# Storing a spectrum by component, mode and line instead of line, component and mode

## The chip, the cores and the metric

The program runs on one core of one Trainium2 chip. The metric is device time in microseconds of one execution of the whole program, from the first to the last instruction. A core has several engines that run side by side, each with its own in-order queue: TensorE (PE in the profile, with its weight loads shown as PEld), VectorE (DVE), ScalarE (ACT), GpSimd (POOL) and SyncE (SP, which here only starts transfers). Engines wait for one another through semaphores. Matmuls read their two operands from the on-chip memory SBUF and write to the accumulators in PSUM; VectorE and ScalarE read and write both.

## The reference, cut to what matters

Four layers follow one another on an input of 4 images of 64 x 64 pixels with 128 channels; each adds its result to its input. The change is in the second one, layer 1 in the code. It normalizes by groups of four channels, takes a real Fourier transform along each of the two image axes, keeps 16 modes, multiplies each mode by its own complex 128 x 128 channel matrix, transforms back, and sends the sum through a two-stage feed-forward with a layer norm:

```python
def _forward_fourier(x, w1, w2):
    xt = jnp.transpose(x, (0, 3, 1, 2))
    ...
    fty = jnp.fft.rfft(xt, axis=-1, norm='ortho')
    f1 = jnp.einsum('bixy,ioy->boxy', fty[..., :nm], cw1)      # nm = 16 modes
    xy = jnp.fft.irfft(jnp.concatenate([f1, pad_y], axis=-1), n=N, axis=-1, norm='ortho')
    ftx = jnp.fft.rfft(xt, axis=-2, norm='ortho')
    f2 = jnp.einsum('bixy,iox->boxy', ftx[:, :, :nm, :], cw2)
    xx = jnp.fft.irfft(jnp.concatenate([f2, pad_x], axis=-2), n=M, axis=-2, norm='ortho')
    return jnp.transpose(xx + xy, (0, 2, 3, 1))
h = _forward_fourier(x, w1, w2)
h1 = jax.nn.relu(jnp.einsum('bmni,ih->bmnh', h, ff_w0) + ff_b0)
h2 = jnp.einsum('bmnh,ho->bmno', h1, ff_w1) + ff_b1
return _layer_norm(h2, ln_g, ln_b)
...
x = x + _L1_conv_ref(_gn(x), L1_conv_w1, L1_conv_w2, ...)
```

## The kernel before, in words

The layers run one after the other. `layer1` loops over the four images and calls `layer1_image` for each. All data is fp32. Layer 0 has a queue of work with due times and layer 2 has a planner, but in layer 1 the order of the work on each engine is that of the program as the tile framework lays it out, with pools of buffers deciding what may run ahead. After the first image the weights of layer 2 are prepared (`layer2_weights`, L744 and following); the framework moves many of these small VectorE operations between those of image 0's second axis.

For one image, `layer1_image` finds the scale `s_` and offset `o_` of the group norm (`group_norm`, transposes at L59), and then does the same for each of the two axes. I call that a half image; there are eight. A line is one of the 64 rows (or columns) of the image. A half image goes like this:

- **Analysis, L641.** 32 matmuls, four to a PSUM tile `pu`. Each takes 128 pixels (two lines) as weights and streams the 96 columns of the transform table `an`, which hold sine, cosine and minus sine of 16 modes for both lines. So a `pu` tile holds eight lines, each with 3 x 16 = 48 values, for 128 channels on the partitions. The three components let one complex product be done as two real matmuls.
- **Write of the spectrum, L642.** ScalarE scales each `pu` tile by `s_` and writes it to `U`. There are eight such writes, straight through: both sides have 384 adjacent floats. `U` has one buffer of the shape line, component, mode.
- **Correction, L645.** VectorE adds eight times the offset to the 64 values of the cosine component of mode 0.
- **Mode products, L653 and L656.** For each of 16 modes two matmuls accumulate in PSUM: the weights are the real and the imaginary channel matrix of this mode, and two components of `U` for all 64 lines stream through, 128 columns. Four modes fill one PSUM tile `pg`.
- **Copy, L659.** VectorE copies `pg` to `G`, in the order line, mode, component. Four copies.
- **Back transform, L665 to L684.** TensorE transposes `G` (L665), ScalarE copies the result (L667), TensorE multiplies it with the synthesis table (L671), and VectorE puts the result into `hT` (L681) or adds it there (L684).

After both axes come the feed-forward (L691, L692, L696) and the layer norm (from L701), in eight blocks of 512 pixels, and the store at L716. The second axis reads the image a second time with the pixels in column order (`xa`, L636).

PSUM tiles come from a pool with two tags, `a` and `b`, of four buffers each. `pu` and `pt` share `a`; `pg`, `ph` and `po` share `b`.

Of the kernel before, what the change touches and what calls it, by code (L numbers as in the profile page):

```python
# [11 lines left out]
F32 = mybir.dt.float32  # L12
AF = mybir.ActivationFunctionType
ALU = mybir.AluOpType
# [3 lines left out]
P = 128  # L18
# [65 lines left out]
def layer0(sh, A, x_in, x_out, scr):  # L84
# [7 lines left out]
    with ExitStack() as ctx:  # L92
# [300 lines left out]
        def products(G, q, hT):  # L393
            U = G["unit"]
            rev = U["rev"]
            qo = 3 - q if rev else q
            e = qo // 2
            if U["yT"][e] is None:
                U["yT"][e] = psy.tile([P, 2, 2 * P], F32, name=f"yT{e}")
                if U["k"] == 0:  # L400
                    for r in range(2):
                        for s in range(2):
                            t0 = (2 * e + r) * P
                            nc.tensor.matmul(
                                U["yT"][e][:, r, s * P : (s + 1) * P],
                                lhsT=U["u"][:, s, t0 : t0 + P],
                                rhs=D_diag[:, s, :],
                                start=(r == 0 and s == 0),
                                stop=False,
                                skip_group_check=True,  # L410
                            )
                    U["started"] |= {(e, j) for j in range(4)}
            for j in range(4):
                jo = 3 - j if rev else j
                nc.tensor.matmul(  # L415
                    U["yT"][e][32 * jo : 32 * jo + 32, qo % 2, :],
                    lhsT=U["Ws"][G["g"]][:, :, 4 * q + j],
                    rhs=hT[:, j, :],
                    start=((e, jo) not in U["started"]),
                    stop=(G["g"] == 3),  # L420
                    skip_group_check=True,
                )
                U["started"].add((e, jo))
            if G["g"] == 3 and q % 2:

                y, k = U["y"], U["k"]
                ye = y[:, 2 * e : 2 * e + 2, :]
                if k == 1:
                    nc.scalar.copy(ye, U["yT"][e])
                else:  # L430
                    nc.vector.tensor_tensor(ye, ye, U["yT"][e], ALU.add)  # L431
                if k == 2:
                    for r in range(2):
                        nc.vector.bn_stats(U["st"][:, 4 * U["pc"] + 2 * e + r, 0, :], y[:, 2 * e + r, :])
                if q == 3:
                    nc.sync.dma_start(U["dst"](k), y)
# [179 lines left out]
def layer1_image(sh, w, pools, x_dram, x_out, x=None):  # L616

    nc = sh.nc
    big, tmp, small, ps = pools
    if x is None:  # L620
        x = big.tile([P, NJ, DM], F32, name="x1")
        load_image(nc, x, x_dram)
    s_, o_ = sh.group_norm(lambda j: x[:, j, :], ps, small, tag="a")
    o8 = small.tile([P, 1], F32, name="o8")
    nc.vector.tensor_scalar(o8, o_, 8.0, None, ALU.mult)

    hT = big.tile([P, NT], F32, name="hT", bufs=1)
    for axis in range(2):

        if axis == 0:  # L630
            xa = x
        else:
            xa = big.tile([P, NJ, DM], F32, name="xa", bufs=1)
            xv = x_dram.rearrange("(h w2 w1) d -> w1 h w2 d", w1=2, w2=32)
            for q in range(2):
                nc.sync.dma_start(xa[64 * q : 64 * q + 64], xv[q])  # L636
        U = tmp.tile([P, 64, 3, 16], F32, name="U1", bufs=1)
        for g in range(NJ // 4):
            pu = ps.tile([P, 4 * 96], F32, name="pu", tag="a")
            for q in range(4):  # L640
                nc.tensor.matmul(pu[:, q * 96 : q * 96 + 96], lhsT=xa[:, 4 * g + q, :], rhs=w["an"], start=True, stop=True)  # L641
            nc.scalar.activation(  # L642
                U[:, 8 * g : 8 * g + 8].rearrange("p l c m -> p (l c m)"), pu, AF.Identity, scale=s_
            )
        nc.vector.tensor_scalar(U[:, :, 1, 0], U[:, :, 1, 0], o8, None, ALU.add)  # L645

        G = tmp.tile([P, 64, 16, 2], F32, name="G1", bufs=1)
        wm = w["w1"] if axis == 0 else w["w2"]
        for g in range(4):
            pg = ps.tile([P, 4, 2, 64], F32, name="pg", tag="b")  # L650
            for q in range(4):
                m = 4 * g + q
                nc.tensor.matmul(  # L653
                    pg[:, q], lhsT=wm[:, m, 0, :], rhs=U[:, :, 1:3, m].rearrange("p l c -> p c l"), start=True, stop=False
                )
                nc.tensor.matmul(  # L656
                    pg[:, q], lhsT=wm[:, m, 1, :], rhs=U[:, :, 0:2, m].rearrange("p l c -> p c l"), start=False, stop=True
                )
            nc.vector.tensor_copy(G.rearrange("p l m c -> p m c l")[:, 4 * g : 4 * g + 4], pg)  # L659

        for g in range(4):
            pt = ps.tile([P, 4, P], F32, name="pt", tag="a")
            for q in range(4):
                l0 = 4 * (4 * g + q)
                nc.tensor.transpose(pt[:, q, :], G[:, l0 : l0 + 4].rearrange("p l m c -> p (l m c)"), sh.ident)  # L665
            GT = tmp.tile([P, 4, P], F32, name="GT1")
            nc.scalar.copy(GT, pt)  # L667
            for q in range(0, 4, 2):
                ph = ps.tile([P, 8, 64], F32, name="ph", tag="b")
                for e in range(2):  # L670
                    nc.tensor.matmul(  # L671
                        ph[:, 4 * e : 4 * e + 4, :].rearrange("p l t -> p (l t)"),
                        lhsT=GT[:, q + e, :],
                        rhs=w["sy"],
                        start=True,
                        stop=True,
                    )
                l0 = 4 * (4 * g + q)
                hv = hT.rearrange("p (h w) -> p h w", w=64)
                if axis == 0:  # L680
                    nc.vector.tensor_copy(hv[:, l0 : l0 + 8, :], ph)  # L681
                else:
                    hv = hv.rearrange("p h w -> p w h")[:, l0 : l0 + 8, :]
                    nc.vector.tensor_tensor(hv, hv, ph, ALU.add)  # L684


    for c in range(NCH):
        h1 = tmp.tile([P, 4, CH], F32, name="h1")
        for f in range(4):
            pf = ps.tile([P, CH], F32, name="pf", tag="a")  # L690
            nc.tensor.matmul(pf, lhsT=w["ff0"][:, f, :], rhs=hT[:, c * CH : (c + 1) * CH], start=True, stop=True)  # L691
            nc.scalar.activation(h1[:, f, :], pf, AF.Relu, bias=w["b0"][:, f : f + 1])  # L692
        po = ps.tile([P, 4, DM], F32, name="po", tag="b")
        for q in range(4):
            for f in range(4):
                nc.tensor.matmul(  # L696
                    po[:, q, :], lhsT=h1[:, f, q * P : (q + 1) * P], rhs=w["ff1"][:, f, :], start=(f == 0), stop=(f == 3)
                )
        row = lambda n: w["rows"][:, n, :].unsqueeze(1).to_broadcast([P, 4, DM])
        h2 = tmp.tile([P, 4, DM], F32, name="h2")  # L700
        nc.vector.tensor_tensor(h2, po, row(0), ALU.add)  # L701
        st = small.tile([P, 4, 6], F32, name="ln_st")
        mv = small.tile([P, 4, 2], F32, name="ln_mv")
        for q in range(4):
            nc.vector.bn_stats(st[:, q, :], h2[:, q, :])
            nc.vector.bn_aggr(mv[:, q, :], st[:, q, :])
        r = sh.rstd(small, mv[:, :, 1], [P, 4], "ln_r")
        for q in range(4):
            nc.vector.tensor_scalar(
                h2[:, q, :], h2[:, q, :], mv[:, q, 0:1], r[:, q : q + 1], ALU.subtract, ALU.mult  # L710
            )
        nc.vector.tensor_tensor(h2, h2, row(1), ALU.mult)
        nc.vector.tensor_tensor(h2, h2, row(2), ALU.add)
        xc = x[:, 4 * c : 4 * c + 4, :]
        nc.vector.tensor_tensor(xc, xc, h2, ALU.add)
        nc.sync.dma_start(x_out[c * CH : (c + 1) * CH, :].rearrange("(j p) d -> p j d", p=P), xc)  # L716


def load_image(nc, x, x_dram):
    for q in range(4):  # L720
        nc.sync.dma_start(
            x[:, 8 * q : 8 * q + 8, :], x_dram[1024 * q : 1024 * q + 1024, :].rearrange("(j p) d -> p j d", p=P)
        )
# [1120 lines left out]
```

## Time and profile before

The time is 8232.35 us, the median of three executions (8224.83, 8232.35, 8241.54).

| | whole program | second layer |
|---|---|---|
| stretch of the span | 0 to 8232.3 us | 6050 to 6610 us |
| TensorE busy | 6551.1 us (80%) | 507.2 us |
| TensorE weight loads | 4166.6 us (51%) | 418.1 us |
| VectorE busy | 6752.2 us (82%) | 294.6 us |
| ScalarE busy | 6192.0 us (75%) | 149.6 us |
| GpSimd busy | 5481.8 us (67%) | 0.0 us |
| mean granted TensorE clock | 0.95 | 0.94 |
| data moved | 142 GB/s | 43 GB/s |

A busy time is a sum over instructions, and matmuls overlap in their pipeline: what one matmul costs in a stream is read from the distance of the starts, not from its length. "PEclk" is the granted clock of TensorE as a share of full speed. "Idle before" says how long an engine stood still before a group of instructions and what released it. A row of the timeline merges instructions that follow one another on one line; "x2" means two records. Each fp32 matmul leaves two records, so a half image has 64 records of mode products.

The layer begins, after a short stretch for the group norm, at TensorE's first analysis matmul at 6050.7 us. In the first half image ScalarE writes the eight parts of U between 6052.8 and 6061.1 us, VectorE corrects mode 0 at 6061.08, the mode products run from 6061.42 to 6075.7, and the fourth G copy follows at 6075.73.

### The profile page before, as it was taken

What the parts mean: (1) busy time and instruction counts of PE and PEld (TensorE: products, weight loads), DVE (VectorE), ACT (ScalarE), POOL (GpSimd) and SP (SyncE); (2) the same over time, 40 slices, a digit from 0 to 9 for tenths busy, and PEclk for the clock granted to TensorE, in tenths of its full rate; (3) what the DMA queues carried; (4) which work ended last, traced back from release to release, by engine and by line L of the source; (5) the groups of instructions that cost most, each with busy time, mean ns of one, the idle gap of its engine ahead of it and who ended that gap; (6) DMA issues with size and microseconds to landing.
All of it is one profiled execution on the core that took longest, in us unless ns stands there. A gap on an engine that the chain in (4) does not pass through costs nothing.

```text
span 8232.3 us, 141196 instructions
## 1 busy us (share of the span) xinstructions
PE 6551.1 (80%) x52976; PEld 4166.6 (51%) x52976; DVE 6752.2 (82%) x7948; ACT 6192.0 (75%) x9798; POOL 5481.8 (67%) x2502
## 2 busy tenths in 40 slices
PE   7788888778888777888887777787778978587689
PEld 3344454444445444444544444454457756474456
DVE  2889999998999999889999999999944554635778
ACT  3899999988898898989988999999822222414567
POOL 0889899998888898888888999999900011020233
PEclk9899999999999999999999999999989989798799
DMA  6445555545555554555555445555541132330332
GB/s 122 158 146 185 162 170 176 162 158 153 183 168 173 179 171 156 159 169 168 173 177 178 163 154 178 177 176 177 174 92 47 25 97 64 83 106 20 108 94 79
DMA packets 1403839, 1165.69 MB, mean 142 GB/s; under 512 B 759829, under 2 KB 1197681, under 8 KB 1336210
## 3 DMA queue, kind: packets, MB, share of 16 engines
q1 hardware_dynamic: 1401474, 1154.93, 45.5%
q8 instruction: 417, 6.83, 0.3%
q14 instruction: 268, 2.20, 0.1%
q10 hardware_dynamic: 1680, 1.74, 0.1%
HBM read 962.66 MB, written 189.74 MB: 140 GB/s over the span
## 4 chain that ended last, share of the span: by engine, by line
PE 21%; DVE 11%; ACT 10%; issue 3%; DMA 2%; POOL 2%; SPq 1%; ACTq 0%; DVEq 0%; POOLq 0%
DVE h L493 5%; ACT hT L390 4%; ACT dA L492 3%; PE pt L380 2%; POOL dB L486 1%; PE po L696 1%; PE pf L691 1%; PE pz L884 1%; PE pt L1527 1%; PE pu L884 1%; DVE in_st L884 1%; PE pb L884 1%; DVE m L884 1%; PE pa L884 1%; PE ps L1581 1%
## 5 line engine op out<-in xcount | busy, mean ns | idle before, releaser
L493 DVE TENSOR_TENSOR_SCAN h<-dA,state,dB 128x512 f32<-128x512 f32 x4096 | 4960.2, 1271 | 340.3 <-ACT dA L492 211.7
L486 POOL TENSOR_TENSOR dB<-du,Bb 128x1024 f32<-128x1024 f32 x2048 | 4816.7, 2386 | 524.5 <-DVE h L493 381.6
L380 PE MATMUL pt<-ident,h 128*128 128x128 f32 x16384 | 2245.1, 281 | 993.4 <-ACT hT L390 988.5
L492 ACT ACTIVATE dA<-delta,A_neg 128x512 f32<-128x512 f32 x4096 | 2746.0, 690 | 166.3 <-DVE h L493 139.4
L380 PEld LDWEIGHTS pt<-ident,h 128*128 128x128 f32 x16384 | 1836.1, 142 | 2029.6 <-ACT hT L390 1783.0
L390 ACT COPY hT<-pt 128x1024 f32<-128x1024 f32 x2048 | 2068.8, 1010 | 187.3 <-PE pt L380 170.8
L415 PE MATMUL yT<-hT,W 128*32 128x256 f32 x16384 | 1394.7, 413 | 2.7 <-DVE y L431 2.1
L884 POOL COPY XG<-Xs 64x9 f32<-64x9 f32 (+2 forms) x44 | 10.9, 293 | 1016.6 <-ACT Xs L884 1016.5
L415 PEld LDWEIGHTS yT<-hT,W 128*32 128x32 f32 x16384 | 454.1, 150 | 350.9 <-issue 333.8
L215 PE MATMUL cv<-xn,taps 128*128 128x512 f32 x1152 | 613.3, 633 | 0.0
L1565 POOL TENSOR_TENSOR S<-S,sm 128x784 f32<-128x784 f32 x128 | 191.1, 1493 | 432.4 <-DVE sm L1563 248.4
L326 PE MATMUL dp<-xd,w_dt 65*128 65x512 f32 x512 | 296.2, 661 | 106.1 <-ACT Ct L313 92.5
L335 POOL TENSOR_TENSOR du<-delta,u 128x1024 f32<-128x1024 f32 x128 | 304.9, 2382 | 66.1 <-DVE delta L332 66.1
L215 PEld LDWEIGHTS cv<-xn,taps 128*128 128x128 f32 x1152 | 183.5, 188 | 234.4 <-issue 233.0
L307 PE MATMUL xd_ps<-u,w_x 128*48 128x512 f32 x512 | 251.1, 614 | 41.3 <-DMA u<-l_xw 16.2
L1572 ACT ACTIVATE S<-S,mx 128x196 f32<-128x196 f32 x512 | 227.9, 448 | 34.8 <-DVE mx L1599 34.2
L692 ACT ACTIVATE h<-pf,b 128x512 f32<-128x512 f32 x128 | 88.0, 687 | 146.6 <-PE pf L691 146.6
L332 DVE SCALAR_TENSOR_TENSOR delta<-delta,dp 128x512 f32<-128x512 f32 x256 | 169.5, 662 | 24.2 <-ACT delta L330 24.2
L326 PEld LDWEIGHTS dp<-xd,w_dt 65*128 65x128 f32 x512 | 78.2, 192 | 218.4 <-ACT Ct L313 151.1
L329 ACT ACTIVATE delta<-dp 128x512 f32<-128x512 f32 x256 | 152.4, 595 | 24.2 <-PE dp L326 19.3
L330 ACT ACTIVATE delta<-delta 128x512 f32<-128x512 f32 x256 | 162.4, 635 | 8.1
L1527 PE MATMUL pt<-ident,S 128*98 128x128 f32 x1024 | 165.3, 286 | 3.3 <-POOL S L1565 1.9
(344 smaller groups left out, 6929.3 us busy)
## 6 DMA issues: line engine op xcount, KB each, us to landing
Bb<-l_B SPq DMA_DIRECT2D x512, 1024.0 KB
W<-l_W SPq DMA_DIRECT2D x512, 256.0 KB
l_y<-y SPq DMA_DIRECT2D x128, 512.0 KB
u<-l_xw SPq DMA_DIRECT2D x64, 512.0 KB
y<-l_y SPq DMA_DIRECT2D x64, 512.0 KB
u<-l_xr SPq DMA_DIRECT2D x64, 512.0 KB
V<-l_v SPq DMA_DIRECT2D x512, 49.0 KB
wr<-wt SPq DMA_DIRECT2D x128, 136.0 KB
```

Source lines behind the costliest of these rows:

```text
L215: nc.tensor.matmul(pm, lhsT=taps[:, s, t, :], rhs=xn[:, dy : dy + 8, dx : dx + 64], start=(t == 0), stop=(t == 8),)
L307: nc.tensor.matmul(xd_ps, lhsT=w_x[:, s, k, :], rhs=u[:, s, :], start=(s == 0), stop=(s == 1))
L326: nc.tensor.matmul(dp, lhsT=w_dt[:, k, s * P : (s + 1) * P], rhs=xd, start=True, stop=True)
L335: nc.gpsimd.tensor_tensor(du, delta, u, ALU.mult)
L380: nc.tensor.transpose(pt[:, j, s, :], G["h"][:, s, t0 : t0 + 32, :].rearrange("p t n -> p (t n)"), sh.ident)
L390: return lambda: nc.scalar.copy(hT, pt.rearrange("p j s d -> p j (s d)"))
L415: nc.tensor.matmul(U["yT"][e][32 * jo : 32 * jo + 32, qo % 2, :], lhsT=U["Ws"][G["g"]][:, :, 4 * q + j], rhs=hT[:, j, :], start=((e, jo) n ...
L486: nc.gpsimd.tensor_tensor(dB, du, B_now[:, q : q + 1, :].to_broadcast([P, 2, CH]), ALU.mult)
L492: nc.scalar.activation(dA, delta[:, s, :], AF.Exp, scale=A_neg[:, k, s, n : n + 1])
L493: nc.vector.tensor_tensor_scan(h[:, s, :, q], dA, dB[:, s, :], state[:, s, n : n + 1], ALU.mult, ALU.add)
L884: r = f(*args, **kw)
L1527: nc.tensor.transpose(pt[:, half, hp, :], U["S"][:, e, hp, 98 * half : 98 * half + 98], sh.ident)
```

## The change

`U` is stored in the order component, mode, line instead of line, component, mode. For one mode, the 64 lines of a component then lie side by side, so each mode product reads two runs of 64 floats, where it read 128 floats that lay 48 floats apart. The correction of mode 0 becomes one run of 64 floats. ScalarE does the reordering: it reads a `pu` tile with 48 floats from one line to the next and writes, for each of 48 pairs of component and mode, a run of eight floats. The change is meant to give the matmuls a contiguous streaming operand. Sizes of tiles, number of instructions and the pools stay.

```diff
-        U = tmp.tile([P, 64, 3, 16], F32, name="U1", bufs=1)
+        U = tmp.tile([P, 3, 16, 64], F32, name="U1", bufs=1)
...
             nc.scalar.activation(
-                U[:, 8 * g : 8 * g + 8].rearrange("p l c m -> p (l c m)"), pu, AF.Identity, scale=s_
+                U.rearrange("p c m l -> p (c m) l")[:, :, 8 * g : 8 * g + 8],
+                pu.rearrange("p (l k) -> p k l", l=8),
+                AF.Identity,
+                scale=s_,
             )
-        nc.vector.tensor_scalar(U[:, :, 1, 0], U[:, :, 1, 0], o8, None, ALU.add)
+        nc.vector.tensor_scalar(U[:, 1, 0, :], U[:, 1, 0, :], o8, None, ALU.add)
...
-                nc.tensor.matmul(
-                    pg[:, q], lhsT=wm[:, m, 0, :], rhs=U[:, :, 1:3, m].rearrange("p l c -> p c l"), start=True, stop=False
-                )
-                nc.tensor.matmul(
-                    pg[:, q], lhsT=wm[:, m, 1, :], rhs=U[:, :, 0:2, m].rearrange("p l c -> p c l"), start=False, stop=True
-                )
+                nc.tensor.matmul(pg[:, q], lhsT=wm[:, m, 0, :], rhs=U[:, 1:3, m, :], start=True, stop=False)
+                nc.tensor.matmul(pg[:, q], lhsT=wm[:, m, 1, :], rhs=U[:, 0:2, m, :], start=False, stop=True)
```

## The prediction

> **What bounds the kernel now.** I read the page first, for the whole span, and then the second layer alone, since the diff touches nothing else. That layer runs from 6050 to 6610 us, 560 of 8232 us. The sums over this stretch come first (columns: length, busy time and instruction count of each engine, granted TensorE clock, busy share of the DMA engines, GB/s):
>
> ```profile
> core 0: us, PE busy (x) PEld busy (x) DVE busy (x) ACT busy (x) POOL busy (x), PEclk, DMA share, GB/s
> 6050.00:6610.00 560.00, 507.21 (x2802) 418.05 (x2802) 294.62 (x751) 149.62 (x260) 0.00 (x0) 0.94 0.20 43
> ```
>
> TensorE is busy for 507 of 560 us, VectorE for 295, ScalarE for 150, and DMA is nearly idle: the layer is bound by TensorE, unlike the kernel as a whole, where VectorE is the busiest. The chain of work that ended last, followed through this stretch only, agrees: the two mode-product lines L653 and L656 hold 11.7% and 11.4% of it, and ScalarE's write of U (L642) 1.0%. So the next view is TensorE's groups there, with mean ns of one instruction:
>
> ```profile
> L696 PE MATMUL po<-ff,h 128*128 128x128 f32 x1024 | 125.0, 275 | 0.1
> L653 PE MATMUL pg<-U,w 128*128 128x128 f32 x256 | 79.2, 398 | 8.0 <-DVE U L645 8.0
> L656 PE MATMUL pg<-U,w 128*128 128x128 f32 x256 | 78.8, 396 | 0.0
> L671 PE MATMUL ph<-c_sy,GT 128*128 128x256 f32 x256 | 61.1, 393 | 1.7 <-ACT GT L667 1.5
> ```
>
> L653 and L696 have one shape: 128x128 weights, 128 columns of fp32. Yet one takes 398 ns and the other 275. A mode product takes as long as L671, which streams 256 columns. What differs is the operand that streams: ff1 is 128 floats in a row, U is read with 48 floats (192 bytes) from each element to the next. Busy times of pipelined matmuls overlap, so for a price I take start to start, from the timeline (start, length, engine, line, operation, count):
>
> ```profile
> 6061.94 0.62 PE L656 MATMUL pg<-U,w 128*128 128x128 f32 x2
> ...
> 6075.08 0.61 PE L656 MATMUL pg<-U,w 128*128 128x128 f32 x2
> ...
> 6130.11 3.06 PE L696 MATMUL po<-ff,h 128*128 128x128 f32 x26
> ```
>
> Between the first two rows lie 30 pairs in 13.14 us: 0.219 us for one record (each fp32 product leaves two). In the last, 26 records take 3.06 us, less 0.275 for the last one's own length over 25 steps: **0.111 us**. The strided read costs a factor of 1.97.
>
> **What the Trainium skill says.** "SBUF — State Buffer", section "Door 1: The DMA port swizzle", says that SBUF has lines of 16 bytes, that two accesses per line are needed for full rate, and that fp32 therefore tolerates a stride of at most four elements. U's stride is 48; the trace agrees in direction, and gives the size, 1.97. The same passage says that PSUM has 8-byte lines and that a non-contiguous PSUM pattern slows matmuls. That could bear on the new ScalarE read of PSUM, but the trace has such a read and shows no cost (below). "TensorE: Matmul & The Clock Gate", section "What's actually happening", says that the array runs at half clock after a window of about 3.4 us with too little activity. The trace agrees: in one-microsecond windows the granted clock drops to 0.50 for some 3.3 us at a time, five times inside mode products.
>
> **The change, part by part.** The instruction streams of the changed kernel have the same instructions, order and waits on every engine; only the shape of the 64 ScalarE writes differs. So all costs are durations.
>
> *Mode products.* Both matmuls now read two runs of 64 adjacent floats, as good as ff1's single run. I price them at 0.111 us. There are 64 records in each of eight half images (four images, two axes): 64 x 0.1074 = 6.87 us each. Is the saving on the path? In the first half image the correction on VectorE (L645) starts at 6061.08 and the last of the four G copies (L659) at 6075.73, 14.65 us later, having waited 2.48 us for TensorE. A copy takes 1.05 us against a new group time of 16 x 0.111 = 1.78, so TensorE still ends last, and the last copy comes 7.78 us after the correction. Nothing beside it hides the saving: 8 x 6.87 = 55.0 us.
>
> One half image is different, the second axis of image 0, where VectorE works on layer 2's weights between the copies (in-order queue, same order after). From the correction at 6094.30 its own work is 2.32 us, then, counted from the start of each copy to the end of what follows it, 2.16, 2.34 and 2.15. With groups ready at 2.37, 4.15, 5.94 and 7.72, the copies start at 2.37, 4.53, 6.87 and 9.02: there VectorE ends last, and 1.3 us of the 6.9 is lost. The loads that this work needs were issued by 6073.6; DMA has finished the burst behind them by about 6084, where the earlier TensorE reaches its first use of the last one, so I add no wait. Sum: **53.7 us**.
>
> *The correction L645* goes from 64 strided to 64 adjacent elements, on the path in every half. It takes 289 ns; a 64x8 operation (L769) takes 0.16 and a contiguous 128x128 one (L779) 0.217, so about 0.19: 8 x 0.1 = 0.8 us.
>
> *ScalarE's write L642* now reads PSUM 48 floats apart and writes runs of eight. The nearest rows, by shape:
>
> ```profile
> L642 ACT ACTIVATE U<-pu,gn_s 128x384 f32<-128x384 f32 x64 | 37.1, 580 | 45.8 <-PE pu L641 45.8
> L884 ACT COPY Zp<-pz 68x512 f32<-68x512 f32 x16 | 9.3, 581 | 143.9 <-PE pz L884 143.9
> L242 ACT COPY xw<-e 128x512 f32<-128x512 f32 x64 | 72.7, 1136 | 13.1 <-DVE e L231 13.1
> ```
>
> Zp does just this: inner runs of eight, read from PSUM 64 floats apart, written adjacent. It takes 581 ns, and the contiguous 512-element copies (L667) 588. So the low bound is 0, and I take it. The high bound is xw, whose strided read is from SBUF: 1136 against about 585, 1.08 ns more per element, or 580 + 384 x 1.08 = 993 ns. TensorE hands over a pu tile every 0.893 us, so a 993 ns write would set the pace: 8 x 0.1 + 0.41 = 1.2 us more on the second axis, 0.4 on the first, where pu starts at half clock. Over four images 6.6 us.
>
> *The clock.* After the mode products TensorE waits 1.1 us for the last G copy. In three of eight half images the transposes and synthesis then ran at half clock: ten transposes took 2.21 to 2.40 us against 1.31, and 16 synthesis records up to 4.44 against 3.72, some 1.6 us each. A window with strided products looks half empty; with dense ones I expect it to stay full clock. The DVE-bound half keeps its gap, so two of the three: **3.0 us**. The opposite bound: the five half-clock stretches inside mode products cost nothing today (0.219 at either clock) but would then cost 1.65 us each, 8.3 us.
>
> Sum: 53.7 + 0.8 + 3.0 = 57.5 us, so 8232.35 - 57.5 = **8175 us**.
>
> **Rivals.** (1) *The half clock stays* at the start of the dense products and before the transposes: 8175 + 8.3 + 3.0 = 8186 us. For it: all four second axes have such a stretch. Against it: they follow a 1 us wait plus strided work, while the dense analysis of these axes just before holds 1.00. (2) *ScalarE's write takes the place of TensorE* as what ends last: 8182 with 993 ns. Were each element to cost four times as much (an assumed factor; 0.836 ns each, from L692's 687 ns for 512 and L642's 580 for 384), a write would take 1.54 us. The eight writes span 8.3 us up to the correction on image 0's first axis and 6.9 on its second, so four images would lose 4 x (16 x 1.54 - 15.2) = 38 us: 8213. For it only the skill's PSUM lines; Zp's 581 is against it. (3) *The stride isn't the limit*, but the weight loads: TensorE's load record for L653 is 220 ns against 192 for L696, and it fills the stretch. Then nothing is saved on TensorE: 8232 if the write is free, 8238 with 993 ns, and **slower**, 8270, with 1.54 us. Against it: L696 loads as many weights and runs at 0.111, so 192 ns loads overlap.
>
> **How the numbers follow.** Forecast 0.76, half clock 0.12, ScalarE 0.08, no gain or slower 0.04. The three executions before spread over 17 us, so a median can move by some 8. Low end: 8175 less 8, and less 3.4 if the two half-clock starts of the feed-forward (5.40 us for eight matmuls against 3.70) go too: about 8163. High end: forecast plus 6.6 for ScalarE and 11.3 for the clock: 8193. Only rival 3 and the dear end of rival 2 lie beyond. Faster by more than 0.2% (16 us) holds in all but rival 3 and the far edge of 2: 0.95; same 0.03; slower 0.02.
>
> **What would show it.** Right: mode-product records of about 275 ns and 0.111 us start to start; the last G copy some 7.8 us after the correction, in one half about 9; L642 near 580 ns; no clock of 0.50 inside the products; the rest of the layer unchanged, some 57 us earlier. Wrong: products still at 0.219, an L642 above 0.89 us, TensorE waiting for ScalarE before each half, or a second and third layer that lose what this one gains.

## The result and the profile after

The changed kernel takes 8177.32 us, the median of four executions (8173.70 to 8181.95), against 8236.64 us for four of the kernel before (8224.83 to 8241.54). The ratio is 0.9931, with a 95% interval from 0.9919 to 0.9943. The forecast was 8175 us with a range from 8163 to 8193.

The sums over the second layer of the changed kernel, 6050 to 6555 us (columns as before):

```profile
core 0: us, PE busy (x) PEld busy (x) DVE busy (x) ACT busy (x) POOL busy (x), PEclk, DMA share, GB/s
6050.00:6555.00 505.00, 447.14 (x2792) 364.98 (x2791) 292.37 (x747) 149.04 (x259) 0.00 (x0) 0.95 0.22 49
```

TensorE lost 60 us of busy time, VectorE and ScalarE almost none. Counted from the first analysis matmul to the start of the last sum on VectorE, the layer shrank from 559.2 us (6050.7 to 6609.9) to 502.5 us (6047.9 to 6550.4), by 56.7 us. The lines are those of the last sum before and after (shortest, median and longest ns, then first and last start) and of the first analysis matmul after:

```profile
L715 DVE TENSOR_TENSOR x<-x,h x32: 675/692/694, 6138.7 to 6609.9; 128x512 f32<-128x512 f32 x32
L714 DVE TENSOR_TENSOR x<-x,h x32: 671/691/693, 6121.9 to 6550.4; 128x512 f32<-128x512 f32 x32
6047.94 9.91 PE L641 MATMUL pu<-c_an,x 128*128 128x96 f32 x64
```

The rest of the 59.1 us between the two profiled executions is the layer's start, 2.8 us earlier, less 0.4 us behind it: in these two executions the layers behind neither added to the gain nor took from it.

The groups that the change touches (L656 and L657 are the old L653 and L656, L658 the old L659, L695 the old L696), and below them the copies before:

```profile
L695 PE MATMUL po<-ff,h 128*128 128x128 f32 x1024 | 125.1, 275 | 0.1
L656 PE MATMUL pg<-U,w 128*128 128x128 f32 x256 | 50.3, 278 | 7.7 <-DVE U L648 7.7
L657 PE MATMUL pg<-U,w 128*128 128x128 f32 x256 | 49.5, 275 | 0.0
L642 ACT ACTIVATE U<-pu,gn_s 128x384 f32<-128x384 f32 x64 | 37.1, 580 | 47.2 <-PE pu L641 47.2
L658 DVE COPY G<-pg 128x512 f32<-128x512 f32 x32 | 33.3, 1042 | 30.5 <-PE pg L657 30.4
```

```profile
L659 DVE COPY G<-pg 128x512 f32<-128x512 f32 x32 | 35.1, 1097 | 82.4 <-PE pg L656 82.4
```

A product record now takes 275 ns, like the feed-forward's L695 of the same shape. ScalarE's write still takes 580 ns, although it reads with a stride and writes runs of eight. The copies waited 82.4 us for TensorE before and wait 30.4 now. Starts are read from the timeline:

```profile
6059.14 0.39 PE L657 MATMUL pg<-U,w 128*128 128x128 f32 x2
...
6065.84 0.39 PE L657 MATMUL pg<-U,w 128*128 128x128 f32 x2
```

That is 30 pairs in 6.70 us, 0.112 us for a record, where it was 0.219.

### The profile page after: what moved, and what is told of

Its sections match the earlier page's. It is cut to its first block, busy times and chain, and to the rows that moved or that the text cites. A ratio compares the mean times of both kernels' runs of the same rounds, so it can differ in the third digit from the quotient of the medians.

```text
span 8173.2 us, 141196 instructions
## 1 busy us (share of the span) xinstructions
PE 6485.2 (79%) x52976; PEld 4114.0 (50%) x52976; DVE 6750.4 (83%) x7948; ACT 6192.5 (76%) x9798; POOL 5484.0 (67%) x2502
## 4 chain that ended last, share of the span: by engine, by line
PE 20%; DVE 11%; ACT 11%; issue 3%; DMA 2%; POOL 2%; SPq 1%; ACTq 0%; DVEq 0%; POOLq 0%
DVE h L493 5%; ACT hT L390 4%; ACT dA L492 4%; PE pt L380 2%; PE po L695 1%; PE pf L690 1%; POOL dB L486 1%; PE pt L1526 1%; PE pu L883 1%; DVE in_st L883 1%; PE pb L883 1%; PE ps L1580 1%; DVE m L883 1%; PE pa L883 1%; PE pz L883 1%
```

## The experiments

**The two halves of the change apart.** The first kernel keeps the old layout and the old contiguous write; only the products' streamed operand becomes dense.

```diff
+        Uf = U.rearrange("p l c m -> p (l c m)")
...
-  ... rhs=U[:, :, 1:3, m].rearrange("p l c -> p c l"), ...
+  ... rhs=Uf[:, 128 * m : 128 * m + 128], ...
...
-  ... rhs=U[:, :, 0:2, m].rearrange("p l c -> p c l"), ...
+  ... rhs=Uf[:, 128 * m + 64 : 128 * m + 192], ...
```

> This kernel keeps the old layout and the old contiguous ScalarE write, and lets each mode product stream 128 adjacent floats of U instead of its own elements, so the products work on the wrong values of the spectrum. Theory (the strided streaming operand is the whole cost, ScalarE's new write is free): product records of 275 ns, 0.111 to 0.112 us start to start, last G copy about 7.8 us after the correction, total near the changed kernel's 8177 us, ratio about 0.993. Rival (ScalarE's strided write costs something in the changed kernel): faster than the changed kernel by some us. Rival (weight loads set the pace): 0.219 us and no gain, ratio 1.000.

Measured: 8177.09 us (four executions, 8172.96 to 8186.82), ratio 0.9937, interval 0.9922 to 0.9951; in this series the kernel before took 8232.18 us, the median of 15. The products run at 0.112 us. This is the changed kernel's time to within the spread, so its new write costs nothing that these runs can see. The weight matrices are read as before, so the rival that weight loads set the pace falls.

The second kernel takes the changed one and goes back to the old way of reading, 48 floats from element to element.

```diff
+        Uo = U.rearrange("p c m l -> p (c m l)").rearrange("p (l c m) -> p l c m", c=3, m=16)
...
-  ... rhs=U[:, 1:3, m, :], ...
-  ... rhs=U[:, 0:2, m, :], ...
+  ... rhs=Uo[:, :, 1:3, m].rearrange("p l c -> p c l"), ...
+  ... rhs=Uo[:, :, 0:2, m].rearrange("p l c -> p c l"), ...
```

> This kernel has the new layout and ScalarE's new write, but the mode products stream elements 48 floats apart, as before the change; they work on the wrong values of the spectrum. Theory: product records of 395 ns, 0.219 us start to start, ScalarE's write still 580 ns, total like the kernel before, ratio 0.999 to 1.001; and TensorE's clock drops to half inside or just after the products in several of the eight half images, as before, since strided products are what makes the windows look empty. Rival (the new write costs): slower than before by 0.1% or more. Rival (the clock drops have nothing to do with the stride): no drops, as in the changed kernel.

Measured: 8232.38 us (twelve executions), ratio 1.0000, interval 0.9992 to 1.0009. Its groups in the second layer:

```profile
L657 PE MATMUL pg<-U,w 128*128 128x128 f32 x256 | 79.2, 398 | 7.7 <-DVE U L648 7.7
L658 PE MATMUL pg<-U,w 128*128 128x128 f32 x256 | 78.8, 396 | 0.0
L642 ACT ACTIVATE U<-pu,gn_s 128x384 f32<-128x384 f32 x64 | 37.2, 581 | 45.0 <-PE pu L641 45.0
```

The whole gain hangs on how TensorE reads, and none of it on how ScalarE writes. The runs also show what becomes of the clock, by the column PEclk over the products of the second axes. First the kernel before, then the changed kernel, then this experiment:

```profile
6094.60:6108.90 14.30, 14.26 (x64) 13.27 (x64) 8.64 (x34) 0.00 (x0) 0.00 (x0) 0.88 0.93 148
```

```profile
6085.10:6092.30 7.20, 7.17 (x64) 7.17 (x64) 7.11 (x26) 0.00 (x0) 0.00 (x0) 1.00 1.07 177
6214.00:6221.20 7.20, 7.15 (x64) 7.15 (x64) 3.16 (x3) 0.00 (x0) 0.00 (x0) 1.00 1.04 180
```

```profile
6106.10:6120.00 13.90, 13.82 (x63) 13.24 (x64) 8.74 (x35) 0.00 (x0) 0.00 (x0) 0.88 0.95 152
6248.50:6262.30 13.80, 13.76 (x63) 13.18 (x64) 3.35 (x3) 0.00 (x0) 0.00 (x0) 0.88 0.96 152
```

A mean of 0.88 over 14 us is one half-clock stretch of some 3.3 us. Counted in one-microsecond windows, the kernel before had five such stretches inside the products and three just behind them, this experiment four and three, together in ten of their 16 half images. The changed kernel and the dense read of the first experiment had none in 16. The waits of about 1 us on either side of the products are there in all four. In the half that VectorE bounds, the wait behind the products even grew from 1.1 to 2.0 us with the change, and the ten transposes behind it lost their half clock all the same (before, then after; the wait stands in brackets):

```profile
6110.00 2.21 PE L665 MATMUL pt<-ident,G 128*128 128x128 f32 x10 [1.11 <-DVE W L847]
```

```profile
6094.56 1.31 PE L664 MATMUL pt<-ident,G 128*128 128x128 f32 x10 [2.02 <-DVE W L846]
```

So the half-clock stretches go with the strided read, as predicted, though six of the 16 strided half images had none. Why they do is not shown. That the stride leaves TensorE with too few useful cycles is an inference, and strided products also last twice as long, which no run varied on its own.

**How large a stride is free.** The changed kernel, with another stride in each half image (8215.07 us in one execution).

```diff
+        step = (1, 2, 3, 4, 6, 8, 16, 48)[2 * b + axis]
...
+            v = Uf[:, 0 : 128 * step].rearrange("p (c l s) -> p c l s", c=2, s=step)
+            return v[:, :, :, (m + c) % step]
```

> The changed kernel with another stride of the streaming operand in each of the eight half images: 1, 2, 3, 4, 6, 8, 16 and 48 floats between neighbours, in this order (the products read wrong values of the spectrum). Theory of 16-byte lines that need two accesses each: 0.112 us start to start for strides 1 and 2, 0.219 for 4 and all larger, stride 3 (1.33 accesses per line) in between, near 0.16. Reading that a stride of up to four floats is free: 0.112 up to 4, then 0.219. Rival (any gap between neighbours costs): 0.219 from stride 2 on. Rival (banks): the price still rises or falls from 6 to 48.

One line for each of the first four strides, 1 to 4 (first column after the count: shortest, median and longest ns of a record, then first and last start):

```profile
L668 PE MATMUL pg<-U,w x32: 275/275/377, 6054.2 to 6061.1; 128*128 128x128 f32 x32
L668 PE MATMUL pg<-U,w x32: 274/274/381, 6080.2 to 6087.3; 128*128 128x128 f32 x32
L668 PE MATMUL pg<-U,w x32: 338/340/426, 6180.8 to 6191.3; 128*128 128x128 f32 x32
L668 PE MATMUL pg<-U,w x32: 405/405/472, 6210.1 to 6224.0; 128*128 128x128 f32 x32
```

Start to start the eight strides take 0.112, 0.113, 0.171, 0.227, 0.227, 0.233, 0.218 and 0.219 us. Two floats are free, three cost half as much again, four and more cost double, with 4% to 7% more at 4 to 8 than at 16 and 48. The higher price of 4 to 8 rests on one half image for each stride.

This fits the two accesses to each line of 16 bytes that the prediction took from the Trainium skill ("SBUF — State Buffer", section "Door 1: The DMA port swizzle"): at a stride of three floats each element takes three quarters of a line, so if the price follows the lines I estimate 2 x 3/4 = 1.5 from that rule, and 1.5 was measured. The same passage lets four fp32 pass as free; here two were, and the measurement decides. A cost that grows with the stride falls too. No half-clock stretch stood in or just behind the products at strides 3, 4 and 8, and five stood there at 6, 16 and 48 together: a strided read can bring such a stretch and need not.

**What ScalarE pays.** The changed kernel, with another form of the write in each half image (8173.48 us in one execution). In the pairs of target and source, `part` is 384 adjacent floats of `U`, `runs` the layout of the change, and `src` the `pu` tile or, in forms 5 to 7, a part of the image in SBUF:

```diff
+  (part, src),
+  (runs, src.rearrange("p (l k) -> p k l", l=8)),
+  (runs.rearrange("p k l -> p l k"), src.rearrange("p (l k) -> p l k", l=8)),
+  (part.rearrange("p (k l) -> p k l", l=8), src.rearrange("p (l k) -> p k l", l=8)),
...
+  (part.rearrange("p (t h) -> p t h", t=2), src.rearrange("p (h t) -> p t h", t=2)),
```

> The changed kernel with another form of ScalarE's 384-element write in each half image (the spectrum is placed wrongly in most): 1 PSUM adjacent to adjacent; 2 PSUM 48 apart to runs of eight, as in the change; 3 PSUM adjacent to single floats 64 apart; 4 PSUM 48 apart to adjacent; 5 SBUF adjacent to adjacent; 6 SBUF 48 apart to adjacent; 7 SBUF adjacent to single floats 64 apart; 8 PSUM 2 apart to adjacent. In 5 to 7 the source is part of the image instead of the transform, so the result of the analysis is left out. Theory (PSUM reads and SBUF writes of ScalarE are free of stride, only a strided SBUF read costs): 580 ns for all but form 6, which takes about 990. Rival (scattered writes cost too): forms 3 and 7 well above 580. Rival (PSUM lines of two floats matter to ScalarE): forms 2, 4 and 8 above 580.

| form | source | target | ns |
|---|---|---|---|
| 1 | PSUM adjacent | adjacent | 582 |
| 2 | PSUM 48 apart | runs of eight | 581 |
| 3 | PSUM adjacent | single floats 64 apart | 920 |
| 4 | PSUM 48 apart | adjacent | 581 |
| 5 | SBUF adjacent | adjacent | 601 |
| 6 | SBUF 48 apart | adjacent | 946 |
| 7 | SBUF adjacent | single floats 64 apart | 916 |
| 8 | PSUM 2 apart | adjacent | 582 |

Form 3's first two writes and the six that follow, in the timeline:

```profile
6179.88 0.91 ACT L657 ACTIVATE U<-pu,gn_s 128x384 f32<-128x384 f32 x1 [1.60 <-PE pu L643]
6181.58 0.92 ACT L657 ACTIVATE U<-pu,gn_s 128x384 f32<-128x384 f32 x1 [0.80 <-PE pu L643]
6183.01 5.37 ACT L657 ACTIVATE U<-pu,gn_s 128x384 f32<-128x384 f32 x6 [0.51 <-PE pu L643]
```

My theory was half right. PSUM may be read 2 or 48 floats apart for nothing, and a strided SBUF read costs, as expected. But scattered single floats cost as much on the SBUF write side. Form 3 is the layout of the change written line by line. Its last six writes start 0.89 us apart, the pace at which TensorE delivers tiles (0.893). Form 7's eight writes of the same kind wait for no tile and start 0.72 us apart:

```profile
6430.88 5.97 ACT L657 ACTIVATE U<-x,gn_s 128x384 f32<-128x384 f32 x8 [0.23 <-DVE gn_s L48]
```

So single floats would not have set the pace either. By my estimate, 920 ns less 581, the last write would have ended 0.34 us later in each half image, and that is what the runs of eight save.

**The same idea in the third layer.** If dense operands pay, other strided ones should be worth changing. Two kernels start from the changed one and alter layouts only. The first stores the tile V of the Gram products pG with adjacent lines:

```diff
-  V = tmp.tile([66, 64, 8], F32, name="V2", tag="S2", bufs=3)
+  V = tmp.tile([66, 8, 64], F32, name="V2", tag="S2", bufs=3)
...
-  nc.scalar.copy(V[:, :, :nr], pv)
+  nc.scalar.copy(V[:, :nr, :], pv.rearrange("p t r -> p r t"))
...
-  Ve = V_last[0][:, :, e]
+  Ve = V_last[0][:, e, :]
```

> The changed kernel, with the same idea in one place of the third layer: the tile V of the Gram products (pG, 256 records, both operands 64 floats that lie 8 apart) is stored row by row, so both operands are dense; ScalarE reads PSUM with a stride and writes runs of 64. Estimate from the trace of the changed kernel: 16 records of pG take 2.18 us, 0.125 us start to start; the dense pz records with as many columns take 0.062. Theory (a strided operand costs double, streaming or as weights): 256 x 0.063 = 16 us less TensorE work, of which what lies on the chain shows: 8161 to 8172 us. Rival (the Gram products are hidden or wait for ScalarE anyway): 8177 us as the changed kernel.

Measured: 8156.07 us (8150.81 to 8158.60), ratio 0.9904, interval 0.9887 to 0.9920; in this series the kernel before took 8234.67 us. A group of 16 pG records in the changed kernel, then here:

```profile
6635.78 2.18 PE L883 MATMUL pG<-V 66*64 66x64 f32 x16
```

```profile
6635.61 1.15 PE L883 MATMUL pG<-V 66*64 66x64 f32 x16
```

From 0.125 to 0.062 us a record (less the last one's own length, over 15 steps), as expected. The total is 21 us lower than the changed kernel's, below the expected 8161 to 8172, while the products account for 16 us. In the traces, counted from the end of the second layer, this kernel starts the third layer's last token mean 16.5 to 20.1 us earlier than the four kernels whose third layer is untouched (before, changed, dense read, ScalarE's forms). These four differ by 3.6 us among themselves, so the products show in full, and how much of the further 5 us is more than spread stays open.

The second kernel also stores U2 by part, row and line, so that the 512 px records load dense weights.

```diff
-  U = large("U2", [P, 64, 2, 32])
+  U = large("U2", [P, 2, 32, 64] if by_mode else [P, 64, 2, 32])
...
-  px[:, e, :], lhsT=U[:, :, q, 4 * g + e], rhs=w["quad"][:, q, :]
+  px[:, e, :], lhsT=U[:, q, 4 * g + e, :], rhs=w["quad"][:, q, :]
```

> The changed kernel, with the spectrum U2 of the third layer's normalized input also stored by part, row, line: its 512 px records take U2 as weights, 64 columns that lie 64 floats apart today, at 0.112 us start to start, and become dense; the Gram products' V is dense too, and pv streams adjacent lines. ScalarE writes U2 in runs of eight floats from a strided PSUM read. Theory (weight loads pay for a stride as the streamed operand does): px near 0.062, 512 x 0.05 = 26 us, plus up to 16 us of pG, most of it on the chain: 8135 to 8155 us. Rival (a strided weight load is hidden, or costs nothing): like the run with V alone. Rival (ScalarE's write of U2 becomes slower): the activation rows of U2 above 584 ns and no gain.

Measured: 8156.71 us (8152.92 to 8158.11), ratio 0.9906, interval 0.9891 to 0.9921: a miss. A group of px in the changed kernel, then here:

```profile
6612.67 5.55 PE L883 MATMUL px<-quad,U 128*64 128x68 f32 x48 [0.67 <-ACT U L883]
```

```profile
6608.97 3.05 PE L883 MATMUL px<-quad,U 128*64 128x68 f32 x48 [0.68 <-ACT U L883]
```

Weight loads do pay for a stride: 0.112 us a record falls to 0.060, and ScalarE's copies of U2 stay at 584 ns on average. But the 26 us of TensorE work do not show. Counted from the end of the second layer, the first image's bias product pbs comes at 136.3 us with V alone and at 130.8 here, and the third layer's last token mean at 1013.8 and 1008.8. So some 5 us are gained by the first image, and the three others add nothing that shows. I take it that their px run beside another image's work; no run shows it. The 5 us were gone at the end of the program. The fourth layer's attention products took 508.5 us from first to last with V alone and 511.3 here, 505.8 in the changed kernel. Whether that is chance stays open: the four executions of each of these kernels spread over 5 to 8 us. Both kernels beat the changed one, and the simpler of them is enough.

## Why the prediction was right, step by step

- *Mode products at 0.111 us.* Right: 0.112. The dense-read and strided-read runs show that the read of the products alone carries the gain.
- *The last G copy 7.78 us after the correction.* Right: 7.76 us (6058.50 to 6066.26), in seven half images.
- *The half that VectorE bounds.* Right in kind, and a little too dear. In image 0's second axis of the changed kernel the four copies follow one another with no wait for TensorE:

```profile
6084.82 0.25 DVE L648 TENSOR_SCALAR U<-U,o 128x64 f32<-128x64 f32 x1 [0.99 <-ACT U L642]
6087.22 1.06 DVE L658 COPY G<-pg 128x512 f32<-128x512 f32 x1
...
6093.51 1.00 DVE L658 COPY G<-pg 128x512 f32<-128x512 f32 x1
```

  The last comes 8.69 us after the correction, where I had 9.02; it lost 0.9 us against the other halves, not 1.3. Products and copies together gave 7 x 6.89 + 5.95 = 54.2 us; the forecast was 53.7 plus the correction's 0.8.
- *The correction at 0.19 us.* Too low: it takes 254 ns where it took 289, so it gave 0.3 us instead of 0.8, which the 54.2 holds. I had interpolated between operations whose sizes don't fix the fixed part.
- *ScalarE's write at no cost.* Right at 580 ns. The Zp row was the right neighbour: a PSUM read with a stride and runs of eight. The xw row, which set the high bound, has a strided SBUF source, and form 6 shows that this is what costs.
- *The clock.* Right in kind, low in size. All three half-clock stretches behind the products went, also that of the half bound by VectorE: ten transposes take 1.31 us in all eight, and the sums of the differences before (0.90 + 1.09 + 1.09 for transposes, 0.72 + 0.39 + 0.46 for synthesis) make 4.7 us. On the path it is less: from the last G copy to the next stage's first matmul, summed over the eight half images, 86.7 us became 82.9. So the term was 3.8 us, where I had 3.0. I had counted on two of the three stretches, because the half bound by VectorE would keep its wait. The wait was there, at 2.0 us, and the stretch went all the same.
- *What I did not count.* Products and copies 54.2 and clock 3.8 make 58.0, and the layer gave 56.7. Of the difference, 1.4 us are in the first axes' analysis, where the time from ScalarE's first write to the correction, summed over four images, went from 33.9 to 35.3 us, as TensorE's half clock at each image's start lasted longer there. The feed-forward's slow starts moved but stayed two (5.40 and 5.26 us against 5.40 twice), which gave back 0.1.

So the near hit of the total, 57.5 forecast and 59.1 between the profiles, rests on right steps: the layer itself gave 56.7, with errors of at most 1.4 us a term that partly cancel. The layer's start, 2.8 us earlier, is chance, as the change touches nothing ahead of it.

## What to carry to other kernels

When two matmuls of one shape have different lengths in the profile, compare how their operands lie in SBUF before anything else. Let ScalarE do the reordering as it empties PSUM: here it read PSUM with a stride for nothing, and its write stayed at 580 ns when it came in runs of eight floats. And ask for each such operand whether its matmuls are on the chain: 16 us of Gram products showed in full, 26 us of px hardly at all.

## What the runs showed of the hardware

Weight loads pay for a stride like the streamed operand, as the last experiment had expected: 64 columns 64 floats apart took 0.112 us a record and 0.060 when adjacent. I had not expected that ScalarE's writes of single floats 64 apart take 920 ns against 582 for 384 elements. A stride of three floats has a price between (0.171 us, 1.5 times), and strides of four to eight cost 4% to 7% more than 16 and 48. And the stride of an operand went with TensorE's clock: none of 16 half images with dense products had a half-clock stretch in or just behind them, and ten of 16 with strided ones had 15 between them.
